# A two-layer decoder on one core: the routed experts' weight loads reordered, and the routing chain moved into the shared expert's second quarter

## The chip, the cores and the metric

The kernel runs on one core of a Trainium2 chip. The metric is the time of one execution of the program on the device, in microseconds. Several runs of a kernel are timed, and their median counts.

## The reference, cut to what matters

The program is a decoder of two layers on x, 8 sequences of 256 tokens of width 256 (2048 tokens in all), all in float32. Everything before the last stage stays as it is, up to layer 1's cross attention. The last stage is a mixture of eight experts, of which each token takes one, beside one shared expert that takes every token:

```
x_aD      = layernorm(x).reshape(2048, 256)
scores_aE = x_aD @ router_DE                       # 8 experts
expert, value = top-1 of scores_aE;  gate = sigmoid(value)
routed    = silu(gate*x_aD @ w1[expert]) * (gate*x_aD @ w3[expert]) @ w2[expert]
shared    = silu(x_aD @ ws1) * (x_aD @ ws3) @ ws2  # inner width 704
x         = x + shared + routed
```

## The kernel before

**The engines.** TensorE (PE) multiplies, VectorE (DVE) and ScalarE (ACT) empty PSUM, GpSimd (POOL) issues the gathers and scatters of rows, and SyncE (SP) issues the transfers of the weights. Each of them runs its own list of instructions in the order in which it was written; one that waits holds up all behind it. Without further words a scheduler sets that order. `tc.manual_schedule(engines=...)` instead pins the listed engines to the order of the code.

**The shared expert.** It works on quarters of 512 tokens. `quarter(q)` computes the hidden layer in six chunks of 128: PE writes h1 and h3 of a chunk (L864), ACT takes the silu (L856), and DVE multiplies into `mid` (L857). `joined(q, mid, i)` multiplies 128 tokens of it with ws2 on PE (L1141, "out<-ws,mid") and adds the sum to x on DVE (L1152). Quarters 0 and 1 run at the end of the cross attention, in its PSUM (tile "hx", two buffers), and leave their hidden layers in `mid_s[0]` and `mid_s[1]`. Between chunks of quarter 1 lie the last sequence's layer norm (`routed_rows`, "xne"), its transposition ("tr") and its scores ("sc", `routed_scores`). Quarter 2 and the `joined` of quarters 0 to 2 belong to the last stage, in the code after the routing chain; quarter 3 comes behind the routed tiles.

**The routing chain.** DVE finds each token's best expert (`best`, `rank`, `first`, `hot`). Two matmuls with ones and with a triangle count the tokens of each expert ("counts", L1194 and L1195). Sixteen additions make running sums (`run`, L1199), a comparison and eight additions give the number of tiles of each expert and where they begin (`over`, `tiles`, `at`, `begin`, `far`). From these come each token's row in the sorted list (`pos_i`, L1250) and each tile's expert (`exp_i`, L1266). For each block j of 128 tokens DVE multiplies the kept `rstd` with the gate (L1273) and writes the gated rows `xg` (L177); POOL then scatters them by `pos_i` (L1275) into `xs` in HBM. DVE's order here is the scheduler's.

**The routed tiles.** Seventeen tiles of 128 sorted rows run in the order 0, 1, 12, 2, 3, 13, 4, 5, 14, 6, 7, 15, 8, 9, 16, 10, 11. Tiles under 12 have one expert, those from 12 on have two halves of 64 rows with an expert each ("pair tiles"). An expert's weights in a tile are called a set here, numbered in that order: tile 0 has set 0, tile 1 set 1, tile 12 sets 2 and 3, tile 2 set 4, and so on up to tile 11 with set 21. A set has two transfers on SP's queue: the first weights w13 (L1313, 1408 KB) and the second ones w2 (L1315, 768 KB). Both pools have four buffers, so set k takes the buffers of set k-4.

`into` multiplies a tile with w13 ("h<-xrT,w", L191) and makes the hidden rows `midr`; `outof` multiplies these with w2 ("out<-w,midr", L1347). `turned` transposes two tiles' rows ("xrp", L1325). PE runs one tile ahead: into(0), into(1), outof(0), into(12), outof(1), into(2), outof(12), ... `fetched(t)` issues a tile's transfers two tiles ahead, w13 and w2 of a set next to each other, so that SP's list reads w13 w2 of set 0, w13 w2 of set 1, w13 w2 of set 2 and so on. Each transfer waits until its buffer is free: w13 for the end of the `into`, w2 for the end of the `outof` that read set k-4. PE is pinned here and SP is not; in the built list SP's loads of the experts' numbers from `exp_i` stand ahead of the fifth set's transfers.

**The end.** After the last tile PE runs quarter 3, while POOL gathers the routed rows back from HBM, and DVE adds these and the last `joined`.

Of the kernel before, what the change touches and what calls it, by code (L numbers as in the profile page):

```python
# [38 lines left out]
P = 128  # L39
# [6 lines left out]
E = 8  # L46
# [23 lines left out]
def plain(ctx: ExitStack, tc: tile.TileContext, a: dict, out: bass.AP, odd_i: bass.AP):  # L70
# [799 lines left out]
    def routed_rows(b, work):  # L870

        xn = work.tile([P, 2, D], F32, tag="xn", name="xne")
        mv, rs = norm_stats([x[:, 2 * b + t, :] for t in range(2)], 1e-5, small, "ln")
        for kept, v in zip(norms[b], (mv, rs)):
            nc.gpsimd.tensor_copy(kept, v)
        for t in range(2):
            normed(xn[:, t, :], x[:, 2 * b + t, :], mv, rs, t)
        transposed(xn, work, mm, "", shared["xnT"][:, :, bass.ts(b, S)])

    def routed_scores(b):  # L880

        ps = mm.tile([P, 2, D], F32, tag="mm", name="sc")
        for t in range(2):
            for c in range(2):
                product(
                    ps[:, t, :E], shared["xnT"][:, c, bass.ts(2 * b + t, P)], shared["router"][:, c, :], c == 0, c == 1
                )
        nc.vector.tensor_copy(sc[:, 2 * b : 2 * b + 2, :], ps[:, :, :E])

# [7 lines left out]
    def null_cross_attention(phase):  # L897
# [180 lines left out]
        for b in range(B):  # L1078
# [4 lines left out]
            else:  # L1083
# [4 lines left out]
                shared["mid_s"] = [ended(late.tile([P, NFC, 2 * S], F32, name=f"mid{i}")) for i in range(2)]  # L1088
                order.enter_context(tc.manual_schedule(engines={mybir.EngineType.PE}))
            if b:  # L1090
                routed_rows(b - 1, work)
# [17 lines left out]
        for i, _ in enumerate(quarter(1)):  # L1109
            if i == 3:  # L1110
                routed_rows(B - 1, work)
            if i == 4:
                routed_scores(B - 1)
        order.close()

# [5 lines left out]
    def token_experts(phase):  # L1121
# [5 lines left out]
        sums = phase.enter_context(tc.tile_pool(name="es", bufs=1, space=PSUM))  # L1127
# [27 lines left out]


        def row(parts, name):
            n = sum(k for k, _, _ in parts)
            i, lo = one.tile([P, n], I32, name=f"{name}_i"), 0
            for k, step, base in parts:  # L1160
                nc.gpsimd.iota(i[:, lo : lo + k], [[step, k]], base=base, channel_multiplier=0)
                lo += k
            f = one.tile([P, n], F32, name=name)
            nc.vector.tensor_copy(f, i)
            return f

        ecol = row([(E, -1, E)], "ecol")
        tcol = row([(PAIRED, 2, 0), (2 * (TILES - PAIRED), 1, 2 * PAIRED)], "tcol")
        jcol = row([(NT, P, P // 2), (NT, P, 0)], "jcol")

        def wide(v):
            return v.unsqueeze(2).to_broadcast([P, NT, E])

        best = one.tile([P, NT], F32, name="best")
        nc.vector.tensor_reduce(best, sc, AX.X, ALU.max)
        rank = one.tile([P, NT, E], F32, name="rank")
        nc.vector.tensor_tensor(rank, sc, wide(best), ALU.is_equal)
        nc.vector.tensor_tensor(rank, rank, ecol.unsqueeze(1).to_broadcast([P, NT, E]), ALU.mult)
        first = one.tile([P, NT], F32, name="first")
        nc.vector.tensor_reduce(first, rank, AX.X, ALU.max)  # L1180
        hot = one.tile([P, NT, E], F32, name="hot")
        nc.vector.tensor_tensor(hot, rank, wide(first), ALU.is_equal)
        gates = one.tile([P, NT], F32, name="gates")
        nc.scalar.activation(gates, best, AF.Sigmoid)


        lower = one.tile([P, P], F32, name="lower")
        nc.gpsimd.affine_select(
            out=lower, in_=ones, compare_op=ALU.is_ge, fill=0.0, base=-1, pattern=[[1, P]], channel_multiplier=-1
        )  # L1190
        hotf = hot.rearrange("p j e -> p (j e)")
        counts = sums.tile([P, 2, NT, E], F32, tag="count", name="counts")
        count, before = counts[:, 0], counts[:, 1]
        nc.tensor.matmul(count.rearrange("p j e -> p (j e)"), ones, hotf, start=True, stop=True)  # L1194
        nc.tensor.matmul(before.rearrange("p j e -> p (j e)"), lower, hotf, start=True, stop=True)  # L1195
        run = one.tile([P, NT + 1, E], F32, name="run")
        nc.vector.memset(run[:, 0, :], 0.0)
        for j in range(NT):
            nc.vector.tensor_tensor(run[:, j + 1, :], run[:, j, :], count[:, j, :], ALU.add)  # L1199

        over = one.tile([P, 2 * E, NT], F32, name="overe")
        for k in range(2):
            nc.vector.tensor_tensor(
                over[:, k * E : (k + 1) * E, :],
                run[:, NT, :].unsqueeze(2).to_broadcast([P, E, NT]),
                jcol[:, k * NT : (k + 1) * NT].unsqueeze(1).to_broadcast([P, E, NT]),
# [4 lines left out]
        at = one.tile([P, E + 1, 2], F32, name="at")  # L1211
        nc.vector.memset(at[:, 0, :], 0.0)
# [5 lines left out]
        nc.vector.tensor_tensor(filled[:, 1:2], full_at[:, E:], all_at[:, E:], ALU.add)  # L1218
        filled_i = one.tile([P, 1], I32, name="filled_i")
        nc.vector.tensor_copy(filled_i, filled[:, 1:2])  # L1220
# [8 lines left out]
        nc.vector.scalar_tensor_tensor(far, pairs, -2.0, far, ALU.mult, ALU.add)  # L1229

# [3 lines left out]
        rank_in, half = run[:, :NT, :], P / 2.0  # L1234
        nc.vector.tensor_tensor(rank_in, rank_in, before, ALU.add)
        ends_at = one.tile([P, 3, E], F32, name="ends_at")
        nc.vector.tensor_scalar(ends_at[:, 0, :], pairs, 2.0 * half, None, ALU.mult)
        nc.vector.tensor_scalar(ends_at[:, 1, :], far, half, None, ALU.mult)
        nc.vector.tensor_scalar(ends_at[:, 2, :], begin[:, 0, :], half, None, ALU.mult)
        left = one.tile([P, NT, E], F32, name="left")  # L1240
        nc.vector.tensor_tensor(left, rank_in, each(ends_at[:, 0, :]), ALU.is_ge)
        nc.vector.tensor_tensor(left, left, each(ends_at[:, 1, :]), ALU.mult)
        nc.vector.tensor_tensor(rank_in, rank_in, each(ends_at[:, 2, :]), ALU.add)
        nc.vector.tensor_tensor(rank_in, rank_in, left, ALU.add)
        nc.vector.tensor_tensor(rank_in, rank_in, hot, ALU.mult)
        pos = one.tile([P, NT], F32, name="pos")
        nc.vector.tensor_reduce(pos, rank_in, AX.X, ALU.add)
        nc.vector.tensor_scalar(pos, pos, TILES * P - 1.0, None, ALU.min)
        pos_i = one.tile([P, NT], I32, name="pos_i")
        nc.vector.tensor_copy(pos_i, pos)  # L1250

        n = PAIRED + 2 * (TILES - PAIRED)
        past = one.tile([P, n, 2, E - 1], F32, name="past")
        for k in range(2):
            nc.vector.tensor_tensor(
                past[:, :, k, :],
                tcol.unsqueeze(2).to_broadcast([P, n, E - 1]),
                begin[:, k, 1:].unsqueeze(1).to_broadcast([P, n, E - 1]),
                ALU.is_ge,
            )  # L1260
        exp_f = one.tile([P, n], F32, name="exp_f")
        nc.vector.tensor_reduce(exp_f, past.rearrange("p n k e -> p n (k e)"), AX.X, ALU.add)
        nc.vector.tensor_scalar(tcol, tcol, filled[:, 0:1], None, ALU.is_ge)
        nc.vector.scalar_tensor_tensor(exp_f, tcol, 1.0 - E, exp_f, ALU.mult, ALU.add)
        exp_i = one.tile([P, n], I32, name="exp_i")
        nc.vector.tensor_copy(exp_i, exp_f)  # L1266

        xg = one.tile([P, NT, D], F32, name="xg")
        puts = []
        landed = mybir.DependencyInfo(mybir.DependencyClass.Sync, mybir.DependencyReason.DATA)  # L1270
        for j in range(NT):
            (mv, rs), t = norms[j // 2], j % 2
            nc.vector.tensor_tensor(rs[:, t : t + 1], rs[:, t : t + 1], gates[:, j : j + 1], ALU.mult)  # L1273
            normed(xg[:, j, :], x[:, j, :], mv, rs, t)
# [11 lines left out]
        for q in range(3):  # L1286
            if q > 1:
                mids.append(quarter(q)[0])
            for i in range(4):
                joined(q, mids[q], i)  # L1290


        low = one.tile([P, 1], F32, name="lowe")
        nc.vector.tensor_reduce(low, fit, AX.X, ALU.min)
        nc.vector.tensor_scalar(low, low, S - 0.5, None, ALU.is_gt)
        fine = mm.tile([P, 2 * D], F32, tag="mm", name="fine")[:, :1]
        nc.tensor.matmul(fine, ones, low, start=True, stop=True)
        nc.vector.tensor_scalar(odd_i, fine, P - 0.5, None, ALU.is_lt)
# [8 lines left out]
        def fetched(t):  # L1307
            sets = []
            for i in [t] if t < PAIRED else [2 * t - PAIRED, 2 * t - PAIRED + 1]:
# [3 lines left out]
                nc.sync.dma_start(w13.rearrange("p c f -> p (c f)"), of[:, : 2 * FIRST])  # L1313
# [45 lines left out]
        def slots(order):  # L1359
# [7 lines left out]
            for i, t in enumerate(order):  # L1367
# [6 lines left out]
                if i + 1 < n:  # L1374
                    ahead = into(order[i + 1], got.pop(0), xrT.pop(0))
# [991 lines left out]
```

## Time and profile before

| | |
|---|---|
| median of 4 runs | 1410.49 us (1409.27 to 1412.56) |
| the profiled execution, its own time | 1410.96 us |
| its span in the profile | 1409.2 us, 1.76 us less than its time |
| PE busy | 1359.4 us, 96% of the span |
| DVE, ACT, POOL busy | 35%, 32%, 28% |
| TensorE clock granted | 0.993 |
| quarter 1's first matmul | at 1152.16 us |
| first weight transfer issued | at 1193.19 us |
| first matmul of the routed tiles | at 1227.66 us |
| first matmul of quarter 3 | at 1369.21 us |

Times within the execution count from the start of the span. In a list in order of time, the two numbers at the head of a row are the start and the length of a run of like instructions; a bracket at its end says how long the engine had been idle before, and what ended that. A float32 matmul counts as two instructions or more. In a table of windows there come, after the length, the busy time of PE, of the weight loads, DVE, ACT and POOL, then the granted clock, the mean share of time in which the 16 DMA engines were busy, and the GB/s that they moved.

### The profile page before, as it was taken

The page shows a single profiled execution, that of the slowest core. Times are in us where ns is not written, and L with a number is a line of the kernel's source. Part 1 is how long each engine was busy: PE and PEld are TensorE (multiplying, and loading weights), DVE is VectorE, ACT ScalarE, POOL GpSimd, SP SyncE. Part 2 cuts the span into 40 slices and gives each one's busy share as a digit, 9 for nine tenths or more (in the row PEclk, how much of TensorE's full clock was granted, in tenths as well). Part 3 has the DMA queues.
Part 4 walks back from the last instruction along what each step waited for, and adds up shares of the span by engine and source line. Part 5 has one row for each costly group of instructions (what it writes and reads, how often), then busy time and mean ns, then how long its engine had stood idle before and what let it go on. Part 6 is the DMA issues. An engine that isn't in the chain of part 4 may idle for free.

```text
span 1409.2 us, 28691 instructions
## 1 busy us (share of the span) xinstructions
PE 1359.4 (96%) x12198; PEld 885.0 (63%) x12198; DVE 498.6 (35%) x1484; ACT 457.0 (32%) x730; POOL 394.8 (28%) x493
## 2 busy tenths in 40 slices
PE   6999999999999999999999999999999999999997
PEld 3666756756766666665565656565565646787874
DVE  5443553553555744420222313221211326221212
ACT  2455444444444344422221313132221211122220
POOL 4332142142033244211241414243241521400004
PEclk9999999999999999999999999999999999999999
DMA  9960000000000006010101011010101011789954
GB/s 310 334 209 16 16 17 9 16 16 1 2 9 2 2 9 218 1 63 16 31 16 46 2 46 31 16 32 16 31 1 31 2 30 35 301 308 372 368 206 122
DMA packets 47068, 116.61 MB, mean 83 GB/s; under 512 B 8416, under 2 KB 30544, under 8 KB 42576
## 3 DMA queue, kind: packets, MB, share of 16 engines
q1 hardware_dynamic: 39056, 92.74, 19.6%
q0 software_dynamic: 5152, 18.89, 3.6%
q10 hardware_dynamic: 2720, 3.02, 0.6%
q8 instruction: 100, 1.64, 0.5%
q14 instruction: 40, 0.33, 0.1%
HBM read 104.00 MB, written 27.93 MB: 94 GB/s over the span
## 4 chain that ended last, share of the span: by engine, by line
PE 82%; DVE 5%; POOL 4%; DMA 3%; issue 1%; ACT 1%; SPq 0%; ACTq 0%; POOLq 0%; DVEq 0%
PE fm L191 12%; PE st L249 9%; PE o L281 9%; PE vps L191 8%; PE h L191 5%; PE wo L191 4%; PE ox L992 4%; PE stx L954 4%; PE out L1141 3%; PE h L864 3%; DMA w<-packs 3%; PE qk L191 2%; PE tr L198 2%; PE out L1347 2%; PE hx L864 2%; PE den L968 2%
## 5 line engine op out<-in xcount | busy, mean ns | idle before, releaser
L281 PE MATMUL o<-pT,padv 128*64 128x256 f32 (+1 forms) x1536 | 171.6, 366 | 1.3 <-POOL pT L261 1.3
L258 ACT ACTIVATE pT<-st 128x1024 f32<-128x1024 f32 (+1 forms) x128 | 110.6, 915 | 88.9 <-PE st L249 87.9
L281 PEld LDWEIGHTS o<-pT,padv 128*64 128x64 f32 x1536 | 103.2, 137 | 52.8 <-issue 10.1
L249 PE MATMUL st<-qm,kT 64*128 64x256 f32 (+1 forms) x1024 | 117.4, 368 | 0.7 <-DVE qm L227 0.6
L191 PE MATMUL fm<-ctxT,wkv_x 128*64 128x256 f32 x1024 | 112.9, 380 | 0.0
L191 PE MATMUL vps<-wkv_x,ctxT 128*64 128x512 f32 x512 | 111.8, 593 | 0.0
L249 PEld LDWEIGHTS st<-qm,kT 64*128 64x128 f32 x1024 | 90.3, 189 | 25.8 <-issue 15.6
L191 PEld LDWEIGHTS fm<-ctxT,wkv_x 128*64 128x64 f32 x1024 | 73.0, 137 | 37.3 <-issue 1.3
L960 POOL TENSOR_TENSOR both<-pTx 128x512 f32<-128x512 f32 x64 | 79.5, 1269 | 58.6 <-ACT pTx L958 33.6
L191 PE MATMUL h<-xrT,w 128*64 128x128 f32 (+1 forms) x1936 | 87.5, 250 | 6.8 <-DMA w<-packs 6.1
L958 ACT ACTIVATE pTx<-stx 128x1024 f32<-128x1024 f32 x64 | 62.0, 1021 | 89.9 <-PE stx L954 89.9
L191 PEld LDWEIGHTS h<-xrT,w 128*64 128x64 f32 x1936 | 84.5, 137 | 10.1 <-DMA w<-packs 6.6
L191 PEld LDWEIGHTS vps<-wkv_x,ctxT 128*64 128x64 f32 x512 | 36.4, 137 | 68.9 <-issue 68.6
L258 ACT ACTIVATE pT<-st,kbias 128x1024 f32<-128x1024 f32 x64 | 67.9, 1112 | 28.8 <-PE st L249 28.7
L173 POOL TENSOR_TENSOR lnrs<-lnve,mhalf 128x2 f32<-128x2 f32 x48 | 34.2, 717 | 147.5 <-DVE lnve L171 95.7
L856 ACT ACTIVATE sl<-h 128x128 f32<-128x128 f32 (+1 forms) x114 | 35.2, 310 | 109.1 <-PE h L191 59.9
L249 PE MATMUL st<-qm,memk 64*128 64x256 f32 x512 | 68.8, 393 | 0.5
L857 DVE TENSOR_TENSOR midr<-sl,h 128x128 f32<-128x128 f32 x102 | 29.3, 287 | 109.1 <-PE h L191 76.1
L954 PE MATMUL stx<-qTx,kTx 64*128 64x256 f32 x512 | 64.3, 391 | 2.5 <-ACT pTx L958 2.5
L168 DVE BATCH_NORM_STATS2 lxst<-yx 128x6 f32<-128x256 f32 x16 | 6.0, 418 | 162.7 <-ACT yx L1052 162.7
L191 PE MATMUL qk<-l_wqkv,xnT 128*64 128x512 f32 x256 | 62.6, 611 | 0.7 <-ACT xnT L201 0.7
L261 POOL TENSOR_SCALAR_AFFINE_SELECT pT<-pT 128x512 f32<-128x512 f32 x64 | 40.0, 645 | 82.0 <-ACT pT L258 78.7
(272 smaller groups left out, 2080.0 us busy)
## 6 DMA issues: line engine op xcount, KB each, us to landing
w<-packs SPq DMA_DIRECT2D x22, 1408.0 KB
w<-packs SPq DMA_DIRECT2D x22, 768.0 KB
rs<-rd SPq DMA_DIRECT2D x16, 512.0 KB
packs<-L_ffn_w_eDF SPq DMA_DIRECT2D x8, 704.0 KB
packs<-L_ffn_w_eDF SPq DMA_DIRECT2D x8, 640.0 KB
packs<-L_ffn_w_eFD SPq DMA_DIRECT2D x8, 640.0 KB
ctxT<-ctx_T SPq DMA_DIRECT2D x8, 512.0 KB
wkv_x<-L_xattn_Wkv POOLq DMA_DIRECT2D x1, 4096.0 KB, 17.4
```

Of the source, the lines that this page charges most:

```text
L191: nc.tensor.matmul(out[h], lhsT[:, h], rhs, start=start, stop=stop, skip_group_check=True)
L249: nc.tensor.matmul(st[:, g, i, :n], kT[rows, c, bass.ts(kt, P)], qm[rows, 2 * mq + i, c, q0:], start=True, stop=True,)
L258: nc.scalar.activation(pT[:, :, :, :n], st[:, :, :, :n], AF.Exp, scale=scale, **kb)
L261: nc.gpsimd.affine_select(out=pT[:, :, :, :P], in_=pT[:, :, :, :P], compare_op=ALU.is_ge, fill=0.0, base=0, pattern=[[0, 2], [0, 2], [1, P ...
L281: nc.tensor.matmul(o[64 * i : 64 * i + 64, mq, q0:], v_pad[:, kt, 4 * c + 2 * mq + i, 2 * g : 2 * g + 2, :], pTs[kt][:, g, i, : S - q0], s ...
L856: nc.scalar.activation(sl, h1, AF.Silu)
L864: nc.tensor.matmul(h, shared["ws13"][:, c, lo : lo + P], shared["xnT"][:, c, bass.ts(q, 2 * S)], start=c == 0, stop=c == 1)
L954: nc.tensor.matmul(st[:, g, kt, :], kT[rows, c, bass.ts(kt, P)], qT[rows, c, :], start=True, stop=True)
L958: nc.scalar.activation(pT, st, AF.Exp, scale=scale)
L960: nc.gpsimd.tensor_tensor(both, pT[:, :, 0, :], pT[:, :, 1, :], ALU.add)
L992: nc.tensor.matmul(o[XD * g : XD * (g + 1), i, :], v[:, kt, 2 * (c2 + i) + g, :], pT[:, g, kt, :], start=kt == 0, stop=kt == 1, skip_group ...
L1141: nc.tensor.matmul(ps, mid[:, i, lo : lo + P], w2[:, i, :], start=i == 0, stop=i == NFC - 1)
```

## The change

It has three parts.

1. **SP's order.** `fetched` becomes `first_weights` and `second_weights`. The second weights of a tile are issued behind the first ones of the next tile, so that the list reads w13 of set 0, w13 of 1, w2 of 0, w13 of 2, w13 of 3, w2 of 1, w13 of 4, w2 of 2, w2 of 3, w13 of 5, w2 of 4, ... SP is pinned, and a set's load from `exp_i` stands right before its w13.
2. **The routing chain.** The tables (`routing_tables`) are made on POOL while the cross attention's last sequence begins. `choices` follows the scores inside quarter 1, and `counted` (the two count matmuls, and a third that was "fine" before) follows quarter 1's last chunk. The sixteen running sums become four additions of doubling distance, and a few steps are merged. In the code the last layer norm stands two chunks earlier, and its transposition and scores one.
3. **Pinned orders.** DVE is pinned as well as PE from quarter 1 to the last `joined` before the tiles. On DVE the steps of the chain alternate with blocks 0 to 3 of the gated rows and the four additions of quarter 0; blocks 4 to 15 follow in one piece, and quarter 2's products come behind them. On PE the four `joined` of quarter 0 now stand ahead of quarter 2. The last `joined` of quarter 2 stands behind the first two tiles' transposition.

```diff
@@ end of null_cross_attention
-        for i, _ in enumerate(quarter(1)):
-            if i == 3:
-                routed_rows(B - 1, work)
-            if i == 4:
-                routed_scores(B - 1)
         order.close()
+        with tc.manual_schedule(engines={mybir.EngineType.PE, mybir.EngineType.DVE}):
+            for i, _ in enumerate(quarter(1)):
+                if i == 1:
+                    xn = routed_norm(B - 1, work)
+                if i == 2:
+                    routed_rows(B - 1, xn, work)
+                if i == 3:
+                    routed_scores(B - 1)
+                    choices()
+            counted()
...
@@ token_experts
-        for j in range(NT):
-            nc.vector.tensor_tensor(run[:, j + 1, :], run[:, j, :], count[:, j, :], ALU.add)
+        order.enter_context(tc.manual_schedule(engines={mybir.EngineType.PE, mybir.EngineType.DVE}))
+        def gated(j):
+            (mv, rs), t = norms[j // 2], j % 2
+            nc.vector.tensor_tensor(rs[:, t : t + 1], rs[:, t : t + 1], gates[:, j : j + 1], ALU.mult)
+            normed(xg[:, j, :], x[:, j, :], mv, rs, t)
+        run, spare, half = route["run"], route["sums"], NT // 2
+        for d in (1, 2, 4, 8):
+            nc.vector.tensor_tensor(
+                spare[:, half:, :], run[:, half:, :], run[:, half - d : half + NT - d, :], ALU.add
+            )
+            run, spare = spare, run
...
+        gated(0)
+        joined(0, mids[0], 0)
...
+        gated(3)
+        joined(0, mids[0], 3)
+        put_rows(3)
+        for j in range(4, NT):
+            gated(j)
+            put_rows(j)
...
+        mids.append(quarter(2)[0])
+        for i in range(4):
+            joined(1, mids[1], i)
+        for i in range(3):
+            joined(2, mids[2], i)
+        order.close()
...
-        def fetched(t):
+        def first_weights(t):
             sets = []
             for i in [t] if t < PAIRED else [2 * t - PAIRED, 2 * t - PAIRED + 1]:
                 e = nc.sync.value_load(exp_i[0:1, i : i + 1], min_val=0, max_val=E - 1)
                 of = packs[bass.ds(e, 1), :, :].rearrange("a p d -> (a p) d")
                 w13 = wts.tile([P, 2, FIRST], F32, tag="w13", name="w13")
                 nc.sync.dma_start(w13.rearrange("p c f -> p (c f)"), of[:, : 2 * FIRST])
+                sets.append((w13, of))
+            return sets
+
+        def second_weights(sets):
+            for i, (w13, of) in enumerate(sets):
                 w2 = wts.tile([P, NFC, D], F32, tag="w2", name="w2")
                 nc.sync.dma_start(w2.rearrange("p c d -> p (c d)"), of[:, 2 * FIRST :])
-                sets.append((w13, w2))
-            return sets
+                sets[i] = w13, w2
...
             for i, t in enumerate(order):
                 now = ahead
                 if i + 2 < n:
-                    got.append(fetched(order[i + 2]))
-                    if i % 2 == 0:
-                        xrT += turned(xr)
-                        xr = [rows(t) for t in order[i + 4 : i + 6]]
+                    sets.append(first_weights(order[i + 2]))
                 if i + 1 < n:
-                    ahead = into(order[i + 1], got.pop(0), xrT.pop(0))
-                outof(t, *now)
+                    second_weights(sets[i + 1])
+                if i + 2 < n and i % 2 == 0:
+                    xrT += turned(xr)
+                    xr = [rows(t) for t in order[i + 4 : i + 6]]
+                if i + 1 < n:
+                    ahead = into(sets[i + 1], xrT[i + 1])
+                outof(t, now, sets[i])
-        with tc.manual_schedule(engines={mybir.EngineType.PE}):
-            slots([0, 1, 12, 2, 3, 13, 4, 5, 14, 6, 7, 15, 8, 9, 16, 10, 11])
+        with tc.manual_schedule(engines={mybir.EngineType.PE, mybir.EngineType.SP}):
+            slots(
+                [0, 1, 12, 2, 3, 13, 4, 5, 14, 6, 7, 15, 8, 9, 16, 10, 11], lambda: joined(2, mids[2], 3)
+            )
```

## The prediction

> **What bounds the kernel now.** The engine summary of the page comes first, then the list of waits for the routed tiles.
>
> ```profile
> PE 1359.4 (96%) x12198; PEld 885.0 (63%) x12198; DVE 498.6 (35%) x1484; ACT 457.0 (32%) x730; POOL 394.8 (28%) x493
> ```
>
> PE is the bound nearly everywhere, so the change can only win what PE idles in the stages that it touches. PE's waits between 1227.5 and 1369.3 us (the routed tiles), and between 1152 and 1227.5 us (quarter 1 up to the tiles):
>
> ```profile
> PE h L191 <- DMA w<-packs: 6.1, 4, 1.9
> PE out L1347 <- issue: 1.0, 1, 1.0
> PE h L191 <- ACT xrT L1327: 0.7, 1, 0.7
> ```
> ```profile
> PE hx L864 <- DVE mid L857: 1.8, 1, 1.8
> PE counts L1194 <- issue: 0.6, 1, 0.6
> PE xrp L1325 <- DVE x L1152: 0.4, 1, 0.4
> ```
>
> Columns are total, times, longest. Four waits for weights make 6.1 us; all others come to 4.5 us. The first 0.7 already belongs to the start of the tiles. Next the order of time on PE and SP around one weight wait (tile 13):
>
> ```profile
> 1261.33 2.76 PE L1347 MATMUL out<-w,midr 128*64 128x256 f32 x24
> 1264.02 0.66 PE L1325 MATMUL xrp<-ident,xr 128*128 128x128 f32 x4
> 1264.61 0.45 PE L191 MATMUL h<-xrT,w 128*64 128x64 f32 x8
> 1266.54 5.12 PE L191 MATMUL h<-xrT,w 128*64 128x64 f32 x168 [1.48 <-DMA w<-packs]
> ```
> ```profile
> 1249.12 0.33 SPq L1313 DMA_DIRECT2D w<-packs  x1
> 1256.70 0.33 SPq L1315 DMA_DIRECT2D w<-packs  x1
> 1257.24 0.33 SPq L1313 DMA_DIRECT2D w<-packs  x1
> 1257.82 0.33 SPq L1315 DMA_DIRECT2D w<-packs  x1
> ```
>
> The pair tile starts on its first half and stops for its second, set 7, whose w13 (third row of SP) was issued at 1257.24 and landed 9.3 us later. Its buffer had been free since the into of tile 12 ended at about 1245.8; it stood behind set 6's w2 at 1256.70, which waits for the outof of tile 12. All four waits are second halves. Last, whether DMA has room:
>
> ```profile
> 1232.70:1345.00 112.30, 105.25 (x1888) 90.36 (x1890) 22.99 (x80) 30.51 (x100) 5.85 (x11) 1.00 0.92 352
> 1259.00:1275.00 16.00, 14.52 (x292) 12.24 (x290) 2.87 (x10) 4.02 (x13) 1.06 (x2) 1.00 1.02 417
> ```
>
> With several transfers queued it moves 417 GB/s; over the whole stretch 352, since the queue runs dry whenever SP waits.
>
> **1. SP's order: 6.1 us.** The built list follows the order in which PE frees buffers and needs data (into 12, outof 1, into 2, outof 12). Set 7's w13 goes out right behind set 6's, when the into of tile 12 ends: some 18 us before its use instead of 7.4, against the 9.3 us that it took with a queue before it. The load of the expert's number before it costs SP 0.7 to 1 us (issues at 1197.70 and 1198.86 are 1.16 apart, those without a load 0.55), and waits together with the engine; two in a row delay set 7 by about 1 us.
>
> Does the queue keep up? The w2 of sets 2 and 3 were loaded before the tiles; now they stand behind set 4's w13, so they come into the stage. From the end of the first into to the last w13 the queue carries 18 w13 of 1.442 MB, 18 w2 (sets 2 to 19) of 0.786, and about 15 result rows and 13 token rows of 0.131: 26.0 + 14.1 + 3.7 = 43.8 MB. The first into ends at 1231.4 (below), data flow some 2 us later, and the last into begins at 1359.12 - 7.3 = 1351.8: 118.4 us. At 417 GB/s they take 105 us, 13 to spare; waits appear under 370. Following the buffers tile by tile, in queue order with 2 us of delay at the start and 2 at the end of each transfer (this gives before's four waits as 1.2 to 1.8 us; they were 1.1 to 1.9), each w13 at 417 lands 6.8 us or more ahead of its into and each w2 9 ahead of its outof. I take 417, since several transfers are always queued; the bound is 352, where 43.8 MB need 124.4 us and 6.0 us of waiting stay. The 1.0 us on "issue" is no weight wait; I leave it (other bound: it goes too).
>
> **2. The front: 1.2 us.** Followed on the engines from 1152.16, with durations of the rows:
>
> - The 1.8 us fall away. DVE stood in the layer norm's statistics until 1159.9 before the first product; pinned, this comes at 1156.6.
> - The transposition now comes after three chunks, at 1162.5. Second product until 1160.7, statistics 1.3, POOL's power 0.8, first normed block 0.4: ready at 1163.3. PE waits **0.8** (bounds 0 and 1.2).
> - The counts' 0.6 falls away: hot is ready at about 1171, quarter 1 ends at 1173.2. Fine's matmul (0.3) only moves.
> - Quarter 0's four out run from 1173.9 at 2.59 each, two PSUM buffers. DVE: doubled sums, comparison and reduction until 1177.4; gates (table load 1.28 plus 0.2) are in by 1176.8. The first addition to x ends at 1178.4, before the third out needs it at 1179.1; the second at 1181.7, with at, begin and far ahead of it, just when the fourth needs it: **0.1**. Quarter 2 begins at 1184.4.
> - On DVE pos_i is ready at 1184.1, exp_i at 1186.6, the fourth addition ends at 1187.5. Then twelve gated blocks, and quarter 2's first product only behind them. Price of a block:
>
> ```profile
> 1178.34 0.29 DVE L1273 TENSOR_TENSOR rstd<-rstd,gates 128x1 f32<-128x1 f32 x3
> 1178.55 0.73 DVE L177 TENSOR_SCALAR xg<-x,mean,rstd 128x256 f32<-128x256 f32 x2
> 1188.24 0.35 DVE L1214 TENSOR_TENSOR at<-at,tiles 128x2 f32<-128x2 f32 x2
> ```
>
> Three independent rstd take 0.29, a step of 0.07; two at, each needing the one before, 0.35, a step of 0.20. A block's xg needs its own rstd, so a block is 0.20 + 0.33 (the step of xg) = 0.53, twelve 6.3; with three small steps the product ends at 1194.8. PE has two buffers each for h1 and h3; the third chunk's h3 could start at 1193.0 and waits **1.8** us. Bounds: 0.40 a block (0.07 + 0.33) gives 0.3, the full durations of 0.63 give 3.1.
>
> The Trainium skill, VectorE: DVE Perf Modes, section "The DRAIN you can't avoid", says that a semaphore between chained operations costs nothing extra. This trace shows 0.13 us for a small one; by the rule a block would cost 0.40, the wait would be 0.3 and the front would gain 2.7 instead of 1.2.
>
> - In place of the 0.4 and 0.7 before the tiles: the last joined stands between transposition and first into, 2.59 us of PE over ACT's 0.58 copy; nothing left.
>
> Idle before 1.8 + 0.6 + 0.4 + 0.7 = 3.5, plus 0.4 of small gaps beside the counts and fine; after 0.8 + 0.1 + 1.8 = 2.7: the front gains 1.2, the tiles begin at 1226.5. Bounds -0.5 (1.2 at the transposition, 3.1 at quarter 2) and 3.5 (0 and 0.3).
>
> Costed at nothing: scatters start nine us earlier (pos_i was ready at 1193.5), so POOL's sixteen at 1.27 end by about 1205 and the rows land by about 1218; PE needs them at 1223. The eleven table steps on POOL, about 2.0 us by the rows of the same kinds at 1176 to 1177.2, lie ahead of "both": the second of these ended at 1110.7, den starts at 1113.14, so 2.4 us cover them (uncovered 0.9 at most, at 0.3 a step). The 23 fewer DVE instructions lie beside PE. The end, quarter 3 and its 40 us, only moves forward.
>
> **The sum.** 6.1 + 1.2 = 7.3 us. The profiled execution took 1410.96, so 1403.7; it lies 0.47 above the median: 1403.2.
>
> **The rivals.**
>
> *The queue does not speed up.* If transfers in flight share the engines evenly instead of going in order, more in flight means that each lands later; the mean stays 352 GB/s, and 6.0 of the 7.3 us return: 1409.2. Against it: even sharing of the four issued from 1256.70 would finish set 7's w13 at about 1269.9 (3.15 MB at 417, then 1.31 MB); order would at 1264.6; it came at 1266.5, nearer to order.
>
> *The front pays more.* Quarter 2's products behind twelve gated blocks, and the additions to x behind chain steps, hold PE another 4 us: 1407.2. For it: all of it stands in line on one engine, where the scheduler had mixed it. Against: only the two tight spots above.
>
> *DMA becomes the bound: slower.* w13, w2, token rows, result rows and PE's own instructions all come through the same 16 engines, and two extra w2 enter the stage. Below 348 GB/s the tiles wait more than the 7.3 us gained (43.8 MB in 125.7 us); at 340 they wait 10.4: 1413.6. Against: rows of 417 whenever the queue is filled.
>
> **How the numbers follow.** Forecast 0.70, sharing 0.10, front 0.12, DMA bound 0.08. This kernel's measurement tells 0.2% (2.8 us) from no change: faster is below 1407.7, slower above 1413.3. A part of the front case counts as the same: faster 0.80, same 0.12, slower 0.08. The low end has both upper bounds: 6.1 + 1.0 + 3.5 = 10.6, so 1399.9; the high end is the mean rate kept, 1409.2.
>
> **What would show it.** Right: no row "PE h <- DMA w<-packs", each second half's w13 within 2 us of the first's, first into near 1226.5, GB/s near 390 through the tiles, one PE wait near 1.8 us in quarter 2 for DVE's mid and one near 0.8 before the transposition. Wrong: weight waits of several us in total, a first into after 1228, or PE waiting for w2.

## The result, and the profile after

The changed kernel takes 1407.3 us (median of 40 runs, 1404.47 to 1410.8) against 1409.09 for the kernel before beside it (61 runs): ratio 0.9986, interval 0.9981 to 0.9991, about 2.0 us less. A gain, but inside the 0.2% that the prediction called no change, and not the 7.3 us forecast.

The profiled execution has a span of 1405.7 us (1407.5 with what lies around it). Its summary of the engines and all of PE's waits from 1100 us on:

```profile
PE 1361.4 (97%) x12198; PEld 886.0 (63%) x12198; DVE 502.9 (36%) x1465; ACT 457.5 (33%) x730; POOL 396.0 (28%) x499
```
```profile
PE h L864 <- DVE mid L857: 2.9, 1, 2.9
PE h L191 <- issue: 1.5, 1, 1.5
PE tr L198 <- DVE xne L177: 0.5, 1, 0.5
PE stx L1017 <- ACT pTx L1021: 0.3, 1, 0.3
PE out L1209 <- DVE x L1220: 0.2, 1, 0.2
```

"PE h <- DMA w<-packs" is gone from the list. What is new is the first row, quarter 2's wait for DVE, predicted at 1.8. And PE's busy time rose by 2.0 us for the same 12198 instructions: in this execution something made matmuls longer.

For each kernel the stage is split in two: the **front**, from quarter 1's first matmul to the routed tiles' first, and the **tiles**, from there to quarter 3's first matmul.

| profile of | front | tiles | both |
|---|---|---|---|
| before | 75.50 | 141.55 | 217.05 |
| changed | 79.25 | 135.53 | 214.78 |
| difference | +3.75 | -6.02 | -2.27 |
| forecast | -1.2 | -6.1 | -7.3 |

So the tiles gave what was forecast, and the front took most of it back. The tiles first: tile 13 on PE, then SP at the same set, then a table of windows of the tiles (length, then PE, PEld, DVE, ACT, POOL busy, clock, DMA share, GB/s).

```profile
1265.66 2.76 PE L1392 MATMUL out<-w,midr 128*64 128x256 f32 x24
1268.35 0.66 PE L1370 MATMUL xrp<-ident,xr 128*128 128x128 f32 x4
1268.94 5.35 PE L191 MATMUL h<-xrT,w 128*64 128x64 f32 x176
```
```profile
1250.10 1.49 SPq L1354 DMA_DIRECT2D w<-packs  x2
1252.93 0.33 SPq L1361 DMA_DIRECT2D w<-packs  x1
```
```profile
1236.00:1348.00 112.00, 110.35 (x2033) 95.83 (x2032) 24.21 (x84) 31.52 (x104) 5.83 (x11) 1.00 0.99 396
```

The pair tile runs its 176 instructions in one piece, where before it stopped after 8 of them. The w13 of sets 6 and 7 leave together (x2 at 1250.10), 18.8 us before the tile begins, and the queue carries 396 GB/s through the tiles instead of 352.

Then the front, PE's order around quarter 2:

```profile
1183.57 8.75 PE L864 MATMUL h<-xnTe,ws 128*128 128x512 f32 x20
1195.25 13.59 PE L864 MATMUL h<-xnTe,ws 128*128 128x512 f32 x24 [2.93 <-DVE mid L857]
1208.68 18.29 PE L1209 MATMUL out<-ws,mid 128*128 128x256 f32 x84
```

Behind the wait, 24 instructions take 13.59 us; quarter 1's 24 of the same shape take 10.57 in this execution. The windows of one microsecond tell why (clock in the column before the last two):

```profile
1193.00:1194.00 1.00, 0.00 (x0) 0.00 (x0) 0.93 (x5) 0.00 (x0) 0.69 (x2) 1.00 1.02 420
1194.00:1195.00 1.00, 0.00 (x0) 0.00 (x0) 0.97 (x5) 0.00 (x0) 0.92 (x1) 0.77 1.07 446
1195.00:1196.00 1.00, 0.75 (x1) 0.50 (x2) 0.79 (x2) 0.60 (x1) 0.78 (x1) 0.50 1.01 406
...
1200.00:1201.00 1.00, 1.00 (x2) 0.35 (x2) 0.00 (x0) 0.00 (x0) 0.72 (x1) 0.50 1.04 435
1201.00:1202.00 1.00, 1.00 (x3) 0.38 (x2) 0.00 (x0) 0.00 (x0) 0.69 (x2) 0.82 1.07 453
1202.00:1203.00 1.00, 1.00 (x3) 0.38 (x3) 0.00 (x0) 0.60 (x1) 0.69 (x2) 1.00 1.01 426
```

While PE waits, its granted clock falls to half, and stays there for 6.8 us (0.77 means that 0.46 of that slice ran at half, 0.82 means 0.36, and six whole slices lie between). 13.59 - 10.57 = 3.0 us are lost in this way, beside the 2.93 of the wait itself. And the wait is longer than forecast because of the gated rows. DVE's order among them, then POOL's:

```profile
1188.80 0.43 DVE L177 TENSOR_SCALAR xg<-x,mean,rstd 128x256 f32<-128x256 f32 x1
1189.15 0.15 DVE L1234 TENSOR_TENSOR rstd<-rstd,gates 128x1 f32<-128x1 f32 x1
1189.34 0.62 DVE L177 TENSOR_SCALAR xg<-x,mean,rstd 128x256 f32<-128x256 f32 x1
1189.88 0.14 DVE L1234 TENSOR_TENSOR rstd<-rstd,gates 128x1 f32<-128x1 f32 x1
```
```profile
1188.91 0.96 POOL L1294 DMA_INDIRECT xs<-xg,pos_i  x1 [0.30 <-DVE rstd L1234]
1190.17 0.96 POOL L1294 DMA_INDIRECT xs<-xg,pos_i  x1 [0.30 <-DVE rstd L1234]
```

The slow xg begin at 1188.07, 1189.34, 1190.60, 1191.86 and 1193.12, every 1.26 to 1.27 us, which is the period of POOL's scatters. So a pair of blocks takes 1.26, a block 0.63, not 0.53. That the scatters are the cause is tried below.

### The profile page after: what moved, and what is told of

It is laid out like the page before. It is cut to its first block, busy times and chain, and to the rows that moved or that the text cites. A ratio compares the mean times of both kernels' runs of the same rounds, so it can differ in the third digit from the quotient of the medians.

```text
span 1405.7 us, 28704 instructions
## 1 busy us (share of the span) xinstructions
PE 1361.4 (97%) x12198; PEld 886.0 (63%) x12198; DVE 502.9 (36%) x1465; ACT 457.5 (33%) x730; POOL 396.0 (28%) x499
## 4 chain that ended last, share of the span: by engine, by line
PE 81%; DVE 6%; DMA 6%; POOL 3%; issue 1%; ACT 1%; SPq 1%; ACTq 0%; DVEq 0%; POOLq 0%
PE fm L191 12%; PE st L249 8%; PE o L281 8%; PE vps L191 8%; PE h L191 6%; PE wo L191 4%; PE ox L1055 4%; PE stx L1017 4%; PE out L1392 3%; PE qk L191 3%; PE hx L864 2%; PE tr L198 2%; PE h L864 2%; PE out L1209 2%; PE den L1031 2%; PE ao L191 2%
```

## The experiments

The first theory: SP's order gives its 6 us, and the front loses most of it again through quarter 2's wait for DVE and the halved clock behind that wait. The rival: the loss has nothing to do with that wait, but comes from elsewhere in the new front, or from the two parts disturbing each other (scatters and weights on the same DMA engines); then taking the wait away or filling it would bring nothing, and the two parts would not add up.

### The two parts alone

SP's order alone is the kernel before with `first_weights` and `second_weights` and SP pinned:

```diff
-            got, xrT = [fetched(t) for t in order[:2]], turned(xr)
+            sets = [first_weights(order[0])]
+            if n > 1:
+                sets.append(first_weights(order[1]))
+            second_weights(sets[0])
+            xrT = turned(xr)
```

> The kernel before with SP's new order alone (part 1). If the parts add up, the four weight waits (6.1 us) go and nothing is paid at the front: about 6 us under before, with no row of PE waiting for the packs, a first into near 1227.7 us and the stretch from there to quarter 3 near 135.5 us instead of 141.5. Rival: in the changed kernel the tiles gained only because the scatters and first weights came earlier too; then several us of weight waits stay here, and the gain is 0 to 3 us.

Measured: 1403.44 us (6 runs) against 1409.86 (22 runs): ratio 0.9962, interval 0.9947 to 0.9977. Tiles 135.74, front 75.52, as before. The first three of its PE waits from 1150 to 1370 us:

```profile
PE hx L864 <- DVE mid L857: 1.8, 1, 1.8
PE h L191 <- issue: 1.5, 1, 1.5
PE h L191 <- ACT xrT L1331: 0.7, 1, 0.7
```

The 1.8 and 0.7 of before are still there, the weights' rows are not. So this order needs nothing of the new front, and the rival falls. The gap on "issue" of 1.5, at 1245 us, is new: before had one of 1.0 at 1299 us, which is 0.4 here. The changed kernel has the 1.5 too.

The front alone is the changed kernel with the old loop of slots (`fetched`, w13 and w2 of a set next to each other; SP not pinned):

```diff
-                    second_weights(sets[i + 1])
...
+                    got.append(fetched(order[i + 2]))
```

> The changed kernel with SP's old order: parts 2 and 3 alone. If the front costs what the two traces say (79.25 us from quarter 1 to the first into instead of 75.50), it is 3 to 4 us slower than before, with four weight waits of about 6 us again. Rival, as predicted: the front by itself gains about 1 us, and the loss of the changed kernel comes only together with the pinned SP order; then it is 0 to 2 us faster than before.

Measured: 1412.14 us (12 runs) against 1409.86: ratio 1.0017 (1.0005 to 1.0029), 2.3 us slower. The four weight waits are back (6.6 us), and the gain that the rival expected did not come. Its profile keeps the clock after the same wait:

```profile
1196.09 10.57 PE L864 MATMUL h<-xnTe,ws 128*128 128x512 f32 x24 [2.94 <-DVE mid L857]
```

So the wait alone doesn't always cost the clock: the front is 76.24 here, 0.74 above before's, and 79.25 with the drop. The 3 to 4 us expected took the drop as the rule. The parts add up within the noise: -6.4 and +2.3 is -4.1 by the medians, and -1.8 to -2.4 was measured for both; the intervals, some 2 us to each side for either part, cover the difference. In the profiles with full clock the stage gives a closer sum: -5.78 (SP's order) and +1.13 (front) make -4.65, and the changed kernel's second profile, below, has -4.87. The tiles (135.53 and 135.74) show no disturbance either.

### The same kernel again

> The changed kernel itself, beside the others on one chip. SP's order alone gained about 6 us and the front alone lost about 2, so the parts make about 4 us under before; the change was measured at 2. Theory (the wait of 2.9 us halves the clock only in some executions): about 2 to 4 us under before, and a part of the runs with a granted clock of 0.990 or less, some 3 us slower than the others. Rival (the slow stretch is always there): all runs near the same time, 2 us under before.

Measured: 1407.63 (12 runs) against 1410.0 (23 runs): ratio 0.9988 (0.9974 to 1.0002). In this profile the same wait left the clock whole:

```profile
1194.31 10.57 PE L864 MATMUL h<-xnTe,ws 128*128 128x512 f32 x24 [2.95 <-DVE mid L857]
```

Front 76.25, tiles 135.93, span 1402.6 instead of 1405.7: two executions of one kernel, whose fronts differ by the 3.0 us of this drop. It leaves a mark in the run's mean granted clock, since 6.8 us at half are 3.4 / 1405 = 0.0024 of it. The last two columns count runs whose mean clock is at or below a mark:

| kernel | wait in quarter 2 (profile) | 0.990 or less | 0.991 or less |
|---|---|---|---|
| before | none (1.8 in quarter 1) | 2 of 45 | 7 of 45 |
| changed (all runs with a recorded clock) | 2.93, 2.95 | 17 of 54 | 26 of 54 |
| front alone | 2.94 | 2 of 12 | 4 of 12 |
| waiting longer (below) | 7.99 | 6 of 9 | 8 of 9 |
| SP alone (1.8 in quarter 1); ten blocks; filler; spread | 0 to 1.7 | 0 of 32 | 0 of 32 |

The changed kernel's runs at 0.990 or less are slower than its others by 2.3 us (medians, 15 of the first 42 runs) and by 5.0 (2 of these 12); some 3 were expected. But the mark is rough. Each profile has other stretches at half clock (from about 20 us, from about 306 us, in some from about 202 us, and at the end), and these move the mean too: the profile of "waiting longer" has the drop in quarter 2 and a mean of 0.991. The table shows that the drop goes with the wait, not in how many executions it comes.

These other stretches also tell what decides between two executions of one kernel. In each of the ten profiles all half-clock stretches start whole multiples of 3.413 us apart (in the changed kernel's first profile at 201.26, 307.08 and 1194.54, which is 31 and then 260 such steps), and those inside the kernel last one step or two. Where the steps lie differs from execution to execution. An early wait of the same length in before and in the changed kernel's second profile, each with two of that execution's own steps:

```profile
202.05 0.44 PE L198 MATMUL tr<-ident,qkr 128*128 128x128 f32 x2 [2.56 <-DVE qkr L380]
199.07:202.48 3.41, 0.85 (x8) 0.61 (x7) 1.49 (x4) 1.41 (x2) 2.19 (x3) 1.00 0.26 79
202.48:205.89 3.41, 3.41 (x33) 1.78 (x34) 1.50 (x2) 1.62 (x3) 0.00 (x0) 0.50 0.00 0
```
```profile
201.44 0.44 PE L198 MATMUL tr<-ident,qkr 128*128 128x128 f32 x2 [2.57 <-DVE qkr L380]
199.76:203.17 3.41, 1.73 (x25) 1.26 (x27) 1.44 (x2) 0.72 (x3) 0.91 (x1) 1.00 0.26 73
203.17:206.59 3.42, 3.42 (x44) 2.12 (x41) 1.54 (x3) 1.35 (x2) 0.00 (x0) 1.00 0.00 0
```

Before's wait lies within one step, which has 2.56 us of idle PE, and the next step runs at half clock. In the other execution the edge of a step divides the wait, 1.68 us is the most in one step, and the clock stays. From 60 us to PE's last matmul, the ten profiles have 17 such drops: the step ahead of each held 2.21 us or more of idle PE, and no step with 2.02 us or less was followed by one. In quarter 2 the changed kernel's step held 2.23 in the first profile and 1.68 in the second, that of the front alone 1.79. (Only the drop near 20 us comes behind steps with 1.8 to 2.1 us of idle, so idle time is not the whole measure.) From these numbers follows an estimate: a wait of 2.93 us, placed by chance, puts more than 2.02 to 2.21 us into one step of 3.41 in 56 to 67% of the cases. No run set the place of the steps on purpose.

### The wait's length: shorter, longer, filled

Three versions of quarter 2. Two of the twelve blocks behind its third chunk:

```diff
-        for j in range(4, NT):
+        for j in range(4, NT - 2):
...
+        for i, last in enumerate(hidden_shared(2, pair, silu)):
+            if i == 2:
+                for j in range(NT - 2, NT):
+                    gated(j)
+                    put_rows(j)
```

> The changed kernel with ten of the twelve gated blocks ahead of quarter 2's first product and two behind its third. A block takes 0.63 us in the trace, so PE should wait 2.9 - 1.3 = 1.7 us. Theory (a wait near 3 us can cost the clock, one of 1.8 or 1.9, as before had, does not): no run with a clock of 0.990, and 1.3 us plus the mean loss of the clock, together 2 to 4 us, under the changed kernel. Rival (any wait in this place with the scatters running costs the clock): the half clock stays in some runs and 1.3 us are gained.

Measured: 1405.14 us (10 runs), ratio 0.9969 (0.9958 to 0.9981); a wait of 1.68, full clock in the profile, and no run at 0.991 or less. It is 2.5 us under the changed kernel beside it, within the 2 to 4 expected.

Thirteen small additions on DVE that nobody uses, ahead of quarter 2:

```diff
+        for _ in range(13):
+            nc.vector.tensor_tensor(spare, run, run, ALU.add)
```

> The changed kernel with thirteen small additions more on DVE (128x192, result not used) ahead of quarter 2's first product, about 0.3 us each: PE waits 2.9 + 4 = about 7 us. Theory (an idle PE loses its clock, depending on how the gap lies in the monitor's steps of 3.4 us; a gap of two steps holds one whole step whatever its place): half clock in every run, 3 to 4 us of slow matmuls beside the 4 us, so 5 to 7 us over the changed kernel. Rival (no tie to the wait): half clock in as many runs as in the changed kernel, 4 us over it.

Measured: 1412.95 us (9 runs), ratio 1.0023 (1.0008 to 1.0037), 5.3 us above the changed kernel beside it. The wait came out at 7.99, one more than meant, and 8 of 9 runs have a mean clock of 0.991 or less, against 26 of 54. The time alone would not part the theory (5 to 7) from the rival (4, or 5 with the longer wait); the clock does. In the profile:

```profile
1199.43 12.63 PE L864 MATMUL h<-xnTe,ws 128*128 128x512 f32 x24 [7.99 <-DVE mid L857]
```

Only 2.06 us lost here: a part of the half-clock stretch passes while PE still waits.

Three matmuls whose result is not used, in the wait, in a PSUM bank of their own, so that PE works while DVE is late and the data come no sooner:

```diff
+            if lo == FF + FF % P + 2 * P:
+                for _ in range(3):
+                    nc.tensor.matmul(
+                        fill, shared["ws13"][:, 0, lo : lo + P], shared["xnT"][:, 0, : 2 * S], start=True, stop=True
+                    )
```

> The changed kernel with three matmuls more on PE (128x512, result not used, 2.6 us of PE) between the third chunk's h1 and its h3, where PE waits 2.9 us for DVE; DVE's order is untouched. Theory (idle PE loses its clock): the h3 starts when it did, the clock stays at 1.0, and the 3.2 us of slow matmuls go: about 3 us under the changed kernel, 5 under before. Rival (traffic lowers the clock): half clock from about 1195 to 1201 us as in the changed kernel, and the same time as it, or more.

```profile
1193.03 2.74 PE L1340 MATMUL fill<-xnTe,ws 128*128 128x512 f32 x6
1196.15 10.57 PE L1344 MATMUL h<-xnTe,ws 128*128 128x512 f32 x24 [0.39 <-DVE mid L857]
```

Measured: 1406.14 us (11 runs), ratio 0.9973 (0.9964 to 0.9982). The chunk still waits for DVE as long as in the changed kernel (front 76.27), the scatters and transfers run as there, and not one of 11 runs has a mean clock of 0.991 or less. So it is PE's idleness, not the late product or the traffic, that costs the clock. The gain over the changed kernel is some 1.8 us by the two ratios (0.9973 and 0.9986, some 1.5 us to each side), not the 3 expected: the expectation took the drop as the rule. 1.8 of the 3.0 us that a drop costs is what a drop in six executions of ten would give, in line with the estimate of 56 to 67%.

### Whether the scatters slow DVE

POOL's scatters can't start before `pos_i`. Here it, and all sixteen `put_rows`, come behind the gated blocks; the blocks themselves are unchanged:

```diff
-        nc.vector.tensor_scalar(pos_i, pos, TILES * P - 1.0, None, ALU.min)
...
+        nc.vector.tensor_scalar(pos_i, pos, TILES * P - 1.0, None, ALU.min)
+        for j in range(NT):
+            put_rows(j)
```

> The changed kernel with pos_i written behind the last gated block instead of ahead of them, so that POOL's scatters begin only after the blocks. In the changed kernel every second gated row took 0.62 us instead of 0.41 to 0.44, at POOL's step of 1.27 us. Theory (a scatter that POOL prepares slows DVE): all blocks at 0.52 to 0.54 us, 6.4 us for twelve instead of 7.5, and PE's wait in quarter 2 at 1.8 to 2.1 us, as predicted for the change. Rival (the weight transfers' writes slow DVE, or the row's own place): blocks as in the changed kernel, wait 2.9 us or more. The tiles may start late here, since the rows are scattered 9 us later.

All gated blocks of the changed kernel and then of this one, durations as shortest/median/longest in ns; below them this one's first scatter and its quarter 2:

```profile
L177 DVE TENSOR_SCALAR xg<-x,mean,rstd x16: 411/440/626, 1176.4 to 1193.8; 128x256 f32<-128x256 f32 x16
```
```profile
L177 DVE TENSOR_SCALAR xg<-x,mean,rstd x16: 411/412/415, 1175.8 to 1191.9; 128x256 f32<-128x256 f32 x16
```
```profile
1192.66 1.14 POOL L1293 DMA_INDIRECT xs<-xg,pos_i  x1 [19.25 <-DVE filled_i L1330]
```
```profile
1193.32 10.57 PE L864 MATMUL h<-xnTe,ws 128*128 128x512 f32 x24 [1.58 <-DVE mid L857]
```

With no scatter beside them all sixteen take 0.41, a block is 0.52, and the wait is 1.58. The rival falls: the weight transfers go out beside the blocks here too (from 1186 us). The rows are in time all the same, with no wait before the tiles. One run: 1403.7 us, front 74.89, tiles 135.75.

### The gated blocks spread over quarter 2

The twelve blocks go behind quarter 2's products, two after each chunk:

```diff
-        for j in range(4, NT):
-            gated(j)
-            put_rows(j)
...
-        mids.append(quarter(2)[0])
+        j = 4
+        for last in hidden_shared(2, pair, silu):
+            for _ in range(2):
+                gated(j)
+                put_rows(j)
+                j += 1
+        mids.append(mid_s[0])
```

> The changed kernel with the twelve gated blocks spread over quarter 2, two behind each chunk's product, in place of standing ahead of the first. Theory (the wait halves the clock): PE does not wait 2.9 us before the third chunk's h3, the granted clock stays at 1.0, and the 3.2 us of slow matmuls go as well: about 6 us under the changed kernel, 8 under before. Rival (the clock falls because of the scatters and weight transfers that run then, not because of the wait): the wait goes, the stretch at half clock stays: about 3 us under the changed kernel, 5 under before.

```profile
1184.60 19.05 PE L864 MATMUL h<-xnTe,ws 128*128 128x512 f32 x44
1203.49 18.29 PE L1209 MATMUL out<-ws,mid 128*128 128x256 f32 x84
```

Quarter 2 runs in one piece at full clock. Front 73.04, tiles 135.65. Measured: 1403.08 us (5 runs) against 1409.86: ratio 0.9956 (0.9942 to 0.9969), 6.2 us by the ratio and 6.8 by the medians. The interval, 4.4 to 8.2, holds both the 8 of the theory and the 5 of the rival; the profile and the mean clocks (0 of 5 runs at 0.991 or less) speak against the rival. It beats before and the changed kernel, but it can't be told from SP's order alone (0.9962), though its stage is 2.6 us shorter (208.69 against 211.27).

## Why the prediction was right or wrong

**SP's order: right, mechanism and size.** Forecast 6.1; the tiles gave 6.02 in the changed kernel and 5.81 with SP's order alone. The rate taken was 417 GB/s and 396 came, but no matmul waited for a weight. The rival of even sharing (352 GB/s kept) falls with the 396 and with the weights' rows, and so does the DMA bound.

**The front: wrong, and that decides the case.** Forecast -1.2 (at worst +0.5), measured +0.75 where the clock holds and +3.75 where it doesn't. Term by term:

- The transposition's wait: forecast 0.8, measured 0.49. The additions: 0.1, measured 0.24.
- Quarter 2's wait: forecast 1.8, measured 2.93. The failed step is the price of a block: 0.53 held only without scatters. The prediction had "Costed at nothing: scatters start nine us earlier" and asked only whether the rows come in time; that they run beside the blocks, and what this does to DVE, was not asked. With the scatters moved off, the wait was 1.58, near the 1.8. The bound of 3.1 did hold, by a price of 0.63 that it had reached in another way.
- The "0.4 of small gaps" were no idle time: PE is busy for 72.04 of before's 75.50 us, so all of its idle time is 3.46, the four waits named.
- PE's busy time itself grew from 72.04 to 72.48 (the profiles with full clock) for nearly the same instructions. One piece shows: the four transpositions take 0.76 behind their wait, 0.60 before.
- Sum with full clock: 1.1 - 0.3 + 0.1 + 0.4 + 0.4 = 1.7 more than forecast; -1.2 becomes +0.5, measured +0.75.

**The halved clock was not in the prediction at all**, in no term and no rival. The 1.8 us at quarter 1 in before had cost none, and the wait was priced by its length alone. It costs 3.0 us when it comes; by the count of runs at 0.991 or less, the gain of the filling matmuls and the estimate from the steps, it comes in about half to two thirds of the executions, so it costs 1.5 to 2 us on average. Of the rivals, "the front pays more" came true, at 1407.2 almost to the figure, but half by another mechanism: it had the additions and quarter 2's products held up by 4 us; the products' part is 1.1 above forecast, and the clock was not in it. That its figure fits is in part luck.

**The Trainium skill on the two points.** VectorE: DVE Perf Modes, "The DRAIN you can't avoid", says that a semaphore between chained operations costs nothing extra; by it a block would have cost 0.40 and the wait would have been 0.3. The blocks without scatters took 0.52 and the wait was 1.58, so here the measurement speaks against taking the step as free; no run parts the semaphore's own price from the wait for the result. TensorE: Matmul & The Clock Gate, "Part 1: The HAM clock gate (the "warmup" mystery)", says that the array's clock falls to half after at least one idle window, and that this window of 3413 ns is free-running and does not start over with the kernel. The traces agree on the window: their half-clock stretches start on steps of 3.413 us, and one and the same wait costs the clock in some executions and not in others. They differ on how idle it must be: 2.21 us without a matmul in a step of 3.41 was enough.

**What stays open.** With full clock the stage is 4.87 us shorter than before (212.18 against 217.05); 1.5 to 2 us of mean clock loss leave 2.9 to 3.4, and 2.0 were measured (1.3 to 2.7). Other kernels with the new front, too, are about 1 to 2 us worse than their stage says (spread: 8.4 less in the stage, 6.2 by the ratio; ten blocks: 6.5 and 4.4; front alone: 1.1 more and 2.3), the one with SP's order alone hardly (5.8 less and 5.4). In the profiles, the stretch from quarter 3's first matmul to the end is 40.4 to 41.5 us with the new front (39.9 in the changed kernel's first profile), against 40.0 and 40.2 for before and SP alone; PE takes the same 29.51 us in all, and the difference arises behind it, where the last outputs are written. Whether that is the cause or only scatter between executions was not settled. Nor was it tried why POOL's scatter slows DVE.

## What to carry to other kernels

Order the transfers of a queue by when buffers come free and data are needed, and price it by the rate of the filled queue; that part was right to 0.1 us in the changed kernel and to 0.3 by itself. When a block of work is pinned in front of a product that TensorE waits for, price the wait by its length and also by what TensorE's clock does behind it: in these profiles waits up to 1.9 us in the stage left the clock whole, and waits of 2.3 to 2.9 us cost it where a step of 3.41 us held 2.21 us or more of them. And a step "costed at nothing" because it starts earlier has to be checked against what it now runs beside: spreading the same blocks behind the products took the wait, the lost clock and 4 us with it. The simplest part, SP's order alone, was worth as much as the best of the whole versions.

## What the runs showed of the hardware

- TensorE's granted clock fell to 0.50 during a wait of 2.93 us, 2.2 us after PE's last matmul (1192.32 to 1194.54), and stayed so for 6.8 us. Behind the waits of 1.6 to 1.9 us in quarters 1 and 2 every profile shows full clock, and 2.74 us of unused matmuls in the place of the long wait kept it whole in the profile, with no run of 11 at a mean clock of 0.991 or less.
- In each of ten profiles the half-clock stretches start whole multiples of 3.413 us apart. From 60 us to PE's last matmul, each of the 17 drops follows a step with 2.21 us or more of idle PE, and no step with 2.02 us or less is followed by one; waits of 2.56 and 2.57 us cost the clock when they lay in one step (before) and not when an edge divided them (the changed kernel's second profile).
- While POOL issues an indirect scatter (0.96 us), VectorE's 128x256 float32 multiplication by a row's scalar takes 0.62 us instead of 0.41, once per scatter; with no scatter beside it, 0.411 to 0.415 sixteen times (one execution).
